# Routing the tokens of a mixture of experts in three units instead of four groups

## The chip, the core and the metric

The kernel is one program on one core of a Trainium2 chip. Its time is the device time of one execution in microseconds (us); 608.5 us is the median of three runs (608.38 to 609.04).

The engines are TensorE (PE, matmuls; its weight loads are listed as PEld), VectorE (DVE), ScalarE (ACT), GpSimd (POOL) and SyncE (SP, which here only issues transfers). Each works through its own list of instructions in order and waits on semaphores for the others.

## The reference: what is computed

Eight sequences of 256 tokens, 128 numbers a token, in fp32, pass four blocks. Each block adds its result to its input and takes a layer norm:

```
x = LN(x + linear_attention(x))      # 16 heads, Taylor features
x = LN(x + two_experts_and_shared(x))# 128 -> 512 -> 128, top 1 of 2
x = LN(x + attention(x))             # 16 heads of 8, rotary, causal softmax
x = LN(x + moe(x))                   # 8 experts, top 2
```

The last block is the one that changes. A gate scores each token for 8 experts; the best two are kept, with a softmax over their two scores. An expert computes `silu(x W1) * (x W2)`, 256 wide, and then `W3` back to 128. The output is the sum of the two experts' answers, weighted.

## The kernel before

**Tiles, groups and slots.** The 2048 tokens are 16 tiles of 128. Four tiles, two sequences, make a group (`NG` = 4 groups of `TG` = 4 tiles). The second half of the program holds the softmax attention, the last three groups of the first experts, and the mixture of experts, whose networks are called the second networks.

**How tokens are routed.** After the attention of a group is normed (`normed1`, L1028), `routed` (L1044) places five pieces: `turn` transposes the group's tokens on PE, `scores` multiplies them with the gate and ranks the 8 scores by comparisons on DVE (`ranks`, L1173), `count` adds up on PE how many tokens each expert has before each token (`counts`, L1227), `places` (L1251) turns this on DVE into a row number for each token and choice and into a list of which expert each tile of rows belongs to, and `chances` (L1201) takes the softmax. `sent` (L1059) then scatters each tile's tokens, once for each of the two choices, with an indirect transfer on POOL (L1062) into a table in DRAM, `slots`. In it the rows of one expert stand together and each expert's part begins at a multiple of 128. n tiles of tokens give 2n tiles of rows, and as many as 7 more are needed for the parts' ends, so the table of a group has `SN = 2*TG + E - 1` = 15 tiles of rows. All 15 are computed whatever the counts are. The tables are filled with zeros at the beginning (`emptied`, L218).

**The second networks.** `networks` (L1322) makes the pieces that compute one table. `rows` (L1340) loads four row tiles from DRAM (256 KB, two such buffers), `turn_in` (L1357) transposes them on PE, `weights` (L1348) loads one expert's first weights, 256 KB, from DRAM for each row tile (five buffers, four ahead; the expert's number is read from the list into a register), `up` (L1372) does the four first matmuls of a row tile and the Silu, and `down` (L1401) the second matmuls for two row tiles (each fp32 matmul is two instructions in the trace). Before step 54 Silu is made from Tanh, and one `up` does one tile; from then on one `up` does two. `down` writes the answers to a table in DRAM. When a group's last `down` is done, `joined` (L1518) places the end: gather each token's two answers with indirect transfers on POOL (L1527), weigh and add them, norm, store. The last group does without answers in DRAM: its rows carry their weight and destination along (`pay`), and one-hot matmuls on PE (`placed_back`, L1458) add them at their tokens.

**The order of the work.** `second_half` (L739) writes the order by hand in steps `s`, six for each sequence's attention, from -14 on. At each step the attention's own matmuls come first (`largest`, `weights`, later `attend1`), then pieces fixed to this step (`at`), then n pieces from a queue, then `at_end` pieces. The queue first holds the first experts' pieces, which are gone at step `FREE` = 24. Networks are put into the queue by `begun` (L1072). Before, group g's are put in at step 12 g + 34, so at 34, 46 and 58, and the last group's at 65:

```
            elif s < LATE:
                n = 2 - s % 2
            elif s < LAST:
                n = -(-left // (LAST - s))
            else:
                n = 3
```

`LATE` is 54 and `LAST` is 65. So from 34 to 53 one and two pieces are taken in turn, from 54 to 64 what is left is spread evenly, and from 65 on three pieces a step of the last group alone. The attention's score matmuls end with step 47. At step 54 the last sequence's attention is turned back, `ended1` (L1006) adds it at 55, and the last group's routing follows at 56 to 64. Up to `LAST` the order of PE, ACT, DVE and SP is this one; POOL's list is made by the framework, which puts a scatter where its row numbers are ready.

Of the kernel before, what the change touches and what calls it, by code (L numbers as in the profile page):

```python
# [21 lines left out]
TG = 4  # L22
# [9 lines left out]
SN = 2 * TG + E - 1  # L32
# [13 lines left out]
C_COS, C_SIN, C_M2, C_M4, C_TRI, C_TWO, C_SEL, C_ONE, C_LOW, C_FULL, C_TILE, C_DEST, C_END = 0, 256, 512, 514, 518, 582, 614, 742, 746, 748, 752, 767, 775  # L46


def shape_constants():
# [22 lines left out]
    c[:, C_FULL : C_FULL + TG] = P * np.arange(TG)  # L72
# [7 lines left out]
def network(  # L80
# [107 lines left out]
    for j in range(4):  # L188
# [19 lines left out]
        dram.tile([SN * P, SW if g == NG - 1 else D], F32, tag=f"slots{g}", name=f"slots{g}")  # L208
        for g in range(NG)
    ]  # L210
    answers = [
        dram.tile([SN * P, D], F32, tag=f"answers{g}", name=f"answers{g}")
        for g in range(NG - 1)
# [4 lines left out]
    def emptied():  # L218
        for t in slots:
            nc.sync.dma_start(  # L220
                t.rearrange("(t p) w -> p t w", p=P),
                empty[:, : t.shape[1]].unsqueeze(1).broadcast_to([P, SN, t.shape[1]]),
            )
# [512 lines left out]
    slot_is, shares = {}, {}  # L736


    def second_half():  # L739
# [266 lines left out]
        def ended1(b):  # L1006
# [18 lines left out]
            if s == 1:  # L1025
                at(slot[0] + 1, normed1, g, spreads(rs[g], f"b{g}"))

        def normed1(g, spread):  # L1028
            pay = None
            if g == NG - 1:  # L1030
                pay = [
                    route.tile([P, TG, SW], F32, tag=f"pay{r}", name=f"pay{g}{r}", bufs=1)
                    for r in range(2)
                ]
                xs[g] = scaled_rows(rs[g], f"b{g}", spread, pay[0][:, :, 0:D])
                nc.scalar.copy(pay[1][:, :, 0:D], xs[g])
            else:
                xs[g] = scaled_rows(rs[g], f"b{g}", spread)
            routed(g, pay, slot[0])
# [4 lines left out]
        def routed(g, pay, s):  # L1044

            turn, scores, chances, count, places = gates(g, xs[g], pay)

            def placed():
                slot_is[g], nets[g] = places()

            late = g == NG - 1
            for i, piece in zip((1, 2, 3, 4, 5) if late else (2, 3, 4, 5, 7), (turn, scores, count, placed, chances)):

                (at if late or piece is not count else at_end)(s + i, piece)
            for t in range(TG):
                at(s + (6 + t // 2 if late else 8 + t), sent, g, pay, t)
            at(s + (9 if late else 12), begun, g)

        def sent(g, pay, t):  # L1059

            for r in range(2):
                i = nc.gpsimd.indirect_dma_start(  # L1062
                    out=slots[g],
                    out_offset=bass.IndirectOffsetOnAxis(
                        ap=slot_is[g][:, t, r : r + 1], axis=0
                    ),
                    in_=pay[r][:, t, :] if pay else xs[g][:, t, :],
                    in_offset=None,
                )
                apart(i, f"slots{g}")  # L1070

        def begun(g):  # L1072
            queue.extend(networks(g, nets[g]))
# [19 lines left out]
        while s < 6 * B or fixed or queue:  # L1093
# [30 lines left out]
            elif s < LATE:  # L1124
                n = 2 - s % 2
# [16 lines left out]
    def gates(g, x3, pay):  # L1142

        got = {}

        def turn():
            dst = route.tile([P, GW], F32, tag="gT", name=f"gT_{g}", bufs=1)
            got["xT"] = transposed(x3, f"g{g}", nc.scalar, dst=dst)

        def scores():  # L1150
            pg = bank(f"pe_{g}")
            for t in range(TG):
# [7 lines left out]
            got["ranks"] = ranks(g, pg)  # L1160

        def count():
            got["counts"] = counts(g, got["ranks"][2])
# [4 lines left out]
            lambda: chances(g, *got["ranks"], pay),  # L1168
            count,
            lambda: places(g, got["counts"], got["ranks"][3]),  # L1170
        )

    def ranks(g, pg):  # L1173
        s = spool.tile([P, TG, E], F32, tag="gs", name=f"gs_{g}")
        nc.vector.tensor_copy(s.rearrange("p t e -> p (t e)"), pg[:, : E * TG])
        shape = [P, TG, E, E]
        other = s.unsqueeze(2).broadcast_to(shape)
        own = s.unsqueeze(3).broadcast_to(shape)
        gt = spool.tile(shape, F32, tag="gt", name=f"gt_{g}", bufs=1)
        nc.vector.tensor_tensor(gt, other, own, ALU.is_gt)  # L1180
        ge = spool.tile(shape, F32, tag="ge", name=f"ge_{g}", bufs=1)
# [5 lines left out]
            cst[:, C_TRI : C_TRI + E * E].unsqueeze(1).broadcast_to([P, TG, E * E]),  # L1187
        )
        nc.vector.tensor_max(gt, gt, ge)
        rank = spool.tile([P, TG, E], F32, tag="rank", name=f"rank_{g}")  # L1190
        nc.vector.tensor_reduce(rank, gt, AX.X, ALU.add)

        chosen = route.tile([P, TG + 1, E], BF16, tag="chosen", name=f"chosen_{g}")
        nc.gpsimd.memset(chosen[:, TG, :], 0.0)
        nc.vector.tensor_single_scalar(chosen[:, 0:TG, :], rank, 2.0, op=ALU.is_lt)
        ranked = route.tile([P, TG, 2, E], F32, tag="ranked", name=f"ranked_{g}")
        for n in range(2):
            nc.vector.tensor_single_scalar(ranked[:, :, n, :], rank, float(n), op=ALU.is_equal)
        return s, rank, chosen, ranked

    def chances(g, s, rank, chosen, ranked, pay):  # L1201
# [509 lines left out]
```

## Time and profile before

| | |
|---|---|
| median of three runs | 608.5 us |
| the profiled execution | 610.6 us |
| its span, first to last instruction | 608.9 us |
| PE busy | 550.6 us, 90% |
| DVE, ACT, POOL busy | 54%, 41%, 25% |
| mean granted clock of PE | 0.954 |
| `up` matmuls, L1384 | 480, 70.1 us busy |
| `down` matmuls, L1408 | 240, 36.8 us busy |
| scatters L1062 and gathers L1527 of the first three groups | 24 and 24, near 1 us each on POOL |
| expert weight loads | 60 of 256 KB |

Times inside the trace count from the first instruction. "Busy" is the union of an engine's instructions in a stretch. Matmuls overlap, so the mean duration of one (300 ns in L1384) is longer than the step from one to the next (146 ns, 70.1 us over 480). The granted clock is the share of full speed that PE's throttle allowed. In a timeline row the bracket holds the idle time before the instruction and what ended it; "issue" is time in which the engine waited for nothing that the profile shows, and "remote" an event whose sender it doesn't know.

### The profile page before, as it was taken

How to read it: one execution, taken by the hardware profiler on the slowest of the kernel's cores; microseconds unless marked ns; L12 is line 12 of the kernel's file. 1: busy time of each engine (PE TensorE's matmuls, PEld its weight loads, DVE VectorE, ACT ScalarE, POOL GpSimd, SP SyncE). 2: the span in 40 equal slices, each digit the busy share in tenths (PEclk: the TensorE clock that was granted, in tenths of full speed). 3: DMA queues.
4: the chain of work that ended last, by engine and by line, in shares of the span. 5: the costliest groups of instructions: out<-in, count | busy, mean ns of one | idle time of the engine just before them, and what ended most of it. 6: DMA issues, size and time to landing. Idle time of an engine off the chain costs nothing.

```text
span 608.9 us, 11095 instructions
## 1 busy us (share of the span) xinstructions
PE 550.6 (90%) x4380; PEld 363.9 (60%) x4380; DVE 329.7 (54%) x773; ACT 251.8 (41%) x370; POOL 152.2 (25%) x185
## 2 busy tenths in 40 slices
PE   8999999999999899999999999789889669667896
PEld 3556666666644544445545554557668559567896
DVE  3364677586662353754655477448636326244464
ACT  4465445545511142344544445254256216034131
POOL 5122211212220210122313113612522540721300
PEclk9899999999998999999899999799889969959999
DMA  9109530232220000000000000402143337547721
GB/s 325 56 2 287 114 71 9 64 72 71 58 82 1 0 2 0 1 1 1 1 1 1 1 1 10 148 23 81 65 135 108 106 124 211 165 138 199 212 58 36
DMA packets 39507, 46.31 MB, mean 76 GB/s; under 512 B 3253, under 2 KB 28488, under 8 KB 38432
## 3 DMA queue, kind: packets, MB, share of 16 engines
q1 hardware_dynamic: 37088, 40.33, 23.6%
q0 software_dynamic: 2080, 4.49, 2.3%
q8 instruction: 35, 0.57, 0.4%
q10 hardware_dynamic: 288, 0.79, 0.4%
q14 instruction: 16, 0.13, 0.1%
HBM read 35.42 MB, written 10.17 MB: 75 GB/s over the span
## 4 chain that ended last, share of the span: by engine, by line
PE 71%; DVE 14%; ACT 5%; issue 5%; another core or an unknown queue 3%; DMA 1%; POOL 0%; DVEq 0%; ACTq 0%
PE pg L1384 8%; PE pf L664 7%; PE ph L646 6%; PE po L516 5%; DVE mx L896 5%; PE py L436 5%; PE sb L933 4%; PE pv L359 4%; PE pd L1408 4%; PE s L397 3%; PE sa L864 3%; PE pa L966 2%; PE pr L793 2%; PE py L444 2%
## 5 line engine op out<-in xcount | busy, mean ns | idle before, releaser
L1384 PE MATMUL pg<-xTs,we 128*128 128x128 f32 x480 | 70.1, 300 | 17.4 <-issue 7.6
L1384 PEld LDWEIGHTS pg<-xTs,we 128*128 128x128 f32 x480 | 64.8, 213 | 21.4 <-issue 8.9
L896 DVE TENSOR_REDUCE mx<-sa 128x4 f32<-128x1024 f32 (+1 forms) x48 | 56.5, 1221 | 30.9 <-PE sa L887 18.7
L945 POOL TENSOR_SCALAR_AFFINE_SELECT pr<-pr 128x512 f32<-128x512 f32 (+1 forms) x48 | 37.7, 794 | 132.1 <-ACT pr L943 132.1
L460 POOL TENSOR_TENSOR y<-y 128x512 f32<-128x512 f32 x32 | 33.3, 1041 | 131.5 <-DVE y L453 103.4
L413 ACT ACTIVATE at<-s,rt_half 128x1536 f32<-128x1536 f32 x32 | 49.1, 1536 | 32.0 <-PE s L405 31.7
L414 DVE SCALAR_TENSOR_TENSOR at<-at,causal 128x1024 f32<-128x1024 f32 x32 | 39.2, 1225 | 40.5 <-ACT at L413 40.3
L943 ACT ACTIVATE pr<-sb 128x1024 f32<-128x1024 f32 x48 | 46.6, 1022 | 27.0 <-PE sb L933 22.4
L933 PE MATMUL sb<-qm,kr 32*128 32x128 f32 (+1 forms) x512 | 36.8, 364 | 11.6 <-DVE mx L896 11.3
L1391 DVE TENSOR_TENSOR hT<-pg,sg 128x512 f32<-128x512 f32 (+1 forms) x24 | 15.4, 645 | 58.0 <-ACT sg L1390 36.1
L1408 PE MATMUL pd<-e,hT 128*128 x240 | 36.8, 292 | 8.4 <-issue 8.0
L436 PE MATMUL py<-at,v 128*64 128x256 f32 x256 | 40.9, 398 | 0.5 <-DVE at L414 0.3
L1390 ACT ACTIVATE sg<-pg 128x512 f32<-128x512 f32 (+1 forms) x24 | 13.4, 561 | 62.4 <-remote 32.9
L933 PEld LDWEIGHTS sb<-qm,kr 32*128 32x128 f32 x512 | 24.3, 197 | 24.6 <-DVE mx L896 22.5
L1408 PEld LDWEIGHTS pd<-e,hT 128*128 128x128 f32 x240 | 32.5, 203 | 9.7 <-issue 8.4
L516 PEld LDWEIGHTS po<-wo_sb,y 128*128 128x128 f32 x256 | 31.8, 191 | 9.7 <-issue 5.7
L664 PE MATMUL pf<-hq,w 128*128 128x512 f32 x72 | 36.5, 597 | 0.0
L516 PE MATMUL po<-wo_sb,y 128*128 128x128 f32 x256 | 33.6, 282 | 1.6 <-DVE y L507 1.6
L359 PE MATMUL pv<-wv,xt 128*128 128x512 f32 x64 | 33.6, 633 | 0.5 <-DVE kT L352 0.5
L1062 POOL DMA_INDIRECT slots<-x_b,slot_i x24 | 23.6, 984 | 30.6 <-DVE nets L1301 24.7
L1527 POOL DMA_INDIRECT yb<-answers,slot_i x24 | 23.1, 963 | 29.8 <-DVE mv_o L289 22.8
L966 PE MATMUL pa<-pr,vaug 128*32 128x128 f32 (+1 forms) x512 | 28.3, 337 | 0.0
(240 smaller groups left out, 962.2 us busy)
## 6 DMA issues: line engine op xcount, KB each, us to landing
we<-in_e SPq DMA_DIRECT2D x60, 256.0 KB
bc<-nr SPq DMA_DIRECT2D x14, 512.0 KB
slots<-empty SPq DMA_DIRECT2D x3, 960.0 KB
answers<-yg SPq DMA_DIRECT2D x21, 128.0 KB
xg<-slots SPq DMA_DIRECT2D x9, 256.0 KB
w<-in_w SPq DMA_DIRECT2D x2, 768.0 KB
xt<-in_xt SPq DMA_DIRECT2D x4, 256.0 KB
x<-in_x SPq DMA_DIRECT2D x4, 256.0 KB
```

The source lines that it names most:

```text
L359: nc.tensor.matmul(pv, xT[:, t * P : (t + 1) * P], wv_sb[:, w], start=True, stop=True)
L413: nc.scalar.activation(at, ps[:, :, 0:SC], AF.Square, bias=rt_half, scale=SQ_SCALE)
L414: nc.vector.scalar_tensor_tensor(at[:, :, 0 : 2 * P], at[:, :, 0 : 2 * P], 0.5, causal.unsqueeze(1).broadcast_to([P, 4, 2 * P]), ALU.add, ...
L436: nc.tensor.matmul(py[o, cc], v[:, 0, w], at[:, i, :].rearrange("p (a q) -> p a q", q=P)[:, 0::2, :], start=True, stop=False,)
L516: nc.tensor.matmul(po, ys[b, c // 2][:, c % 2, q * P : (q + 1) * P], wo_sb[:, c, :], start=(c == 0), stop=(c == 7),)
L664: nc.tensor.matmul(got["o"], w2_sb[:, k * P : (k + 1) * P], hq.pop(n), start=(n == 0), stop=(n == 11),)
L896: nc.vector.tensor_reduce(mx[:, 2 * h : 2 * h + 2, 3 * js.start : 3 * js.stop - 2 : 3], ps[h].rearrange("p i (j k) -> p i j k", j=js.stop ...
L933: nc.tensor.matmul(ps[i // 2][:, i % 2, jj * wd : (jj + 1) * wd], kT[r, j, k], qms[b][r, j // 3, q], start=True, stop=True,)
L943: nc.scalar.activation(w, ps[h], AF.Exp)
L966: nc.tensor.matmul(pa[r, jj, :] if m == 0 else pa[r, jj, P:T], va[:, t + m, 4 * i + j, :], prs[b, jp][:, i, jj * T : (jj + 1) * T] if m == ...
L1384: nc.tensor.matmul(ph[:, b, cw], w[:, cw], x, start=True, stop=True)
L1408: nc.tensor.matmul(po[:, a * P : (a + 1) * P], hT[m][:, a, c * P : (c + 1) * P], e3_sb[:, bass.ds(net_i, 1), c * D : (c + 1) * D].rearrang ...
```

## The change

The mixture is routed in three units of 6, 6 and 4 token tiles: the sequences 0 to 2, 3 to 5, and 6 and 7. Tables have 19, 19 and 15 row tiles. As norms come by group, the work up to the ranks, and the ends, are done in five parts: group 0; the first half of group 1 (both unit 0); the second half of group 1; group 2 (both unit 1); group 3 (unit 2). Each part has its own gate transposes, scores, ranks and chances; counts and places come once a unit, when its last part is ranked; each part has its own gathers, sums, norm and store.

In steps: unit 0's last sequence is normed at step 28, counted at the end of 32, placed at 33 and put into the queue at 40. Unit 1's is normed at 46, counted at the end of 49, placed at 50, and put in at 55. Unit 2 goes as group 3 went. The pacing has a new bound `SECOND` = 55: unit 0's 34 pieces are spread evenly over steps 40 to 54, and from 55 what is left is spread to `LAST` as before.

```diff
+PARTS = [(0, 0, 0, 4, 0), (0, 1, 0, 2, 4), (1, 1, 2, 2, 0), (1, 2, 0, 4, 2), (2, 3, 0, 4, 0)]
+UT = [sum(n for v, _, _, n, _ in PARTS if v == u) for u in range(3)]
+SNS = [2 * n + E - 1 for n in UT]
...
-            if s == 1:
-                at(slot[0] + 1, normed1, g, spreads(rs[g], f"b{g}"))
+            for p, (_, pg, t0, n, _) in enumerate(PARTS):
+                if pg == g and t0 + n == 2 * s + 2:
+                    r = rs[g][:, t0 : t0 + n, :]
+                    at(slot[0] + 1, normed1, p, r, spreads(r, f"b{p}"))
...
-            late = g == NG - 1
-            for i, piece in zip((1, 2, 3, 4, 5) if late else (2, 3, 4, 5, 7), (turn, scores, count, placed, chances)):
-
-                (at if late or piece is not count else at_end)(s + i, piece)
-            for t in range(TG):
-                at(s + (6 + t // 2 if late else 8 + t), sent, g, pay, t)
-            at(s + (9 if late else 12), begun, g)
+            late = u == 2
+            full = off + n == UT[u]
+            when = (1, 2, 5, 3, 4) if late else (1, 2, 6, 3, 4) if u == 1 and full else (2, 3, 7, 4, 5)
+            for i, piece in zip(when, (turn, scores, chances)):
+                at(s + i, piece)
+            if not full:
+                return
+
+            (at if late else at_end)(s + when[3], count)
+            at(s + when[4], placed)
+            tiles = [(q, t) for q, part in enumerate(PARTS) if part[0] == u for t in range(part[3])]
+            for i, (q, t) in enumerate(tiles):
+                at(s + (6 + i // 2 if late else 5 + i // 2 if u == 1 else 6 + i), sent, q, pay, t)
+            at(s + (9 if late or u == 1 else 12), begun, u)
...
-            elif s < LATE:
-                n = 2 - s % 2
+            elif s < SECOND:
+                n = -(-left // (SECOND - s))
...
             if m == n_pairs - 1:
-                joined(g)
+                for p, part in enumerate(PARTS):
+                    if part[0] == unit:
+                        joined(p)
...
         s = slot[0]
-        if s < LATE:
-            s += 3
-            places, sums = (0, 1, 2, 3), (6, 6, 7, 7, 8)
+        if unit == 0:
+            s += 1 + off
+            places, sums, end = (0, 1, 2, 3), (4, 4, 5, 5, 6), 1
         else:
 
-            s = max(s + 1, LATE + 10)
-            places = (0, 0, 0, 0) if g == 1 else (0, 0, 1, 1)
-            sums = (1, 1, 1, 1, 1) if g == 1 else (4, 4, 4, 5, 5)
+            s = max(s + 1, LATE + 10) + off // 2
+            places, sums, end = ((0, 0), (3, 3, 3), 2) if off == 0 else ((0, 0, 1, 1), (4, 4, 5, 5, 5), 2)
         later(s, begin)
         later(s + sums[0], opened)
-        for t in range(TG):
+        for t in range(n):
             later(s + places[t], gathered, t)
             later(s + sums[t], summed, t)
         later(s + sums[-1], spread)
         later(s + sums[-1] + 1, scaled)
-        later(s + sums[-1] + (1 if s < LATE else 3), stored)
+        later(s + sums[-1] + end, stored)
...
+    SECOND = LATE + 1
```

The rest of the diff replaces groups by units or parts in names, shapes and tables: `gates`, `ranks` and `chances` take a part of n tiles, `counts`, `places` and `networks` a unit, and constants grow from 775 to 781 columns.

## Prediction

> **What bounds the kernel now.** I read the table of the engines first: TensorE (PE) is busy 90% of the span, the next engine 54%. Then I cut the second half into stages with the table of stretches, using the order of matmuls to place the program's steps: step 24 starts at 359.5 us, 30 at 391.7, 34 at 405.5, 40 at 433.1, 50 at 469.0, 54 at 479.7, 55 at 489.1, and the last group's own networks (step 65) at 558.3. These are eight of the nine rows of that answer; columns are PE, weight load, DVE, ACT, POOL, then the granted clock, the DMA share and GB/s.
>
> ```profile
> 391.70:405.50 13.80, 12.85 (x131) 7.23 (x129) 6.72 (x11) 5.59 (x8) 3.58 (x5) 0.99 0.13 39
> 405.50:433.10 27.60, 25.86 (x281) 19.45 (x277) 23.10 (x69) 14.61 (x23) 6.15 (x8) 0.94 0.24 70
> 433.10:480.80 47.70, 41.92 (x472) 33.23 (x469) 24.33 (x84) 21.61 (x39) 18.00 (x22) 0.96 0.38 112
> 480.80:499.00 18.20, 9.53 (x58) 8.79 (x57) 1.63 (x4) 3.15 (x6) 11.78 (x12) 0.78 0.31 88
> 499.00:518.20 19.20, 19.20 (x148) 18.93 (x148) 12.83 (x49) 11.95 (x22) 0.03 (x1) 0.85 0.78 225
> 518.20:558.30 40.10, 27.89 (x194) 25.84 (x193) 13.73 (x39) 9.95 (x19) 15.59 (x16) 0.83 0.63 176
> 558.30:576.80 18.50, 13.90 (x103) 13.04 (x102) 8.66 (x29) 5.88 (x10) 7.63 (x8) 0.91 0.59 168
> 576.80:608.90 32.10, 25.51 (x225) 25.00 (x223) 19.16 (x59) 8.13 (x14) 0.00 (x0) 0.97 0.21 60
> ```
>
> Steps 30 to 33 have no network pieces beside the attention and still keep PE busy 12.85 of 13.8 us; where pieces are added, the steps grow by about what these cost. So a piece taken out of any stage is worth its PE time. The exceptions are 480.8 to 499.0 (PE 9.5 of 18.2 us) and 518.2 to 558.3 (27.9 of 40.1). In both, POOL issues 16 indirect transfers back to back at 1.28 us each, and the others stand: the timeline shows PE and ACT resuming as POOL's run ends, and the list of waits has ACT's Silu waiting for something that the profile can't name.
>
> ```profile
> 494.96 0.97 POOL L1527 DMA_INDIRECT yb<-answers,slot_i  x1 [0.30 <-issue]
> ...
> 497.61 0.60 ACT L1390 ACTIVATE sg<-pg 128x512 f32<-128x512 f32 x1 [11.67 <-remote]
> ```
> ```profile
> ACT sg L1390 <- remote: 32.9, 5, 11.7
> ```
>
> I asked for the same columns over each of the five runs of indirect transfers (8, 8, 16, 16 and 8 of them):
>
> ```profile
> 378.30:390.40 12.10, 7.90 (x93) 5.37 (x92) 5.32 (x11) 2.56 (x5) 9.20 (x10) 0.78 0.47 153
> 430.90:443.00 12.10, 9.99 (x121) 7.58 (x119) 5.30 (x13) 1.79 (x5) 9.08 (x10) 0.92 0.20 67
> 475.60:497.00 21.40, 12.79 (x93) 11.37 (x93) 3.16 (x9) 3.01 (x5) 15.74 (x16) 0.86 0.37 108
> 518.20:541.00 22.80, 12.23 (x79) 10.52 (x78) 5.14 (x14) 1.40 (x4) 15.59 (x16) 0.80 0.45 128
> 561.20:574.20 13.00, 10.06 (x69) 9.56 (x70) 3.97 (x12) 3.58 (x7) 7.62 (x8) 0.87 0.58 164
> ```
>
> Span less PE busy gives PE's idle time: 4.2, 2.1, 8.6, 10.6 and 2.9 us. A run of 8 costs 3.1 on average and one of 16 costs 9.6, so each transfer past the eighth costs (9.6 - 3.1) / 8 = 0.81 us. By this line a run of 12 costs 6.3 and one of 24 costs 16.1. I use the line as a rule of this trace without knowing its cause.
>
> The Trainium skill speaks against that reading: "SBUF — State Buffer", section "Who interferes with whom", says that DMA never contends with a compute engine. By it the runs would cost nothing and their rearrangement neither; the measured 8.6 and 10.6 us decide here.
>
> **The change, part by part.** *Fewer tiles.* A unit of n token tiles needs 2n + 7 network tiles: 19 + 19 + 15 = 53 in place of 4 x 15 = 60. Prices at full clock, start to next start in the timeline: one `up` 0.95 us, a tile's `down` 0.47, its transpose 0.14, so 1.56 a tile and 10.9 for seven; by the page's whole groups (70.1/480 x 8 + 36.8/240 x 4 + 0.15) it is 1.93 and 13.5. The stages below spend this saving; it isn't added to them.
>
> *Steps 24 to 39 (359.5 to 433.1).* Before, the first group's networks start at step 34; now they start at 40, since unit 0 waits for the third sequence. Out go 6 `up` and 3 transposes of 4 tiles with a wait of 0.7 and half-clock time: -8.8. The first group's run of 8 goes (-4.2), a run of 12 comes at step 33 (+6.3). Gates: transposes and scores are the same 16 tiles in all, in five parts; the fifth part adds 17 DVE instructions of 0.2 to 0.4 us, two parts being half as wide, against one fewer set of counts and places (13 of 0.2). The attention's matmuls (PE 12.85 of 13.8) hide most; I take +0.2, and +3 if that cover fails. Sum -6.5.
>
> *Steps 40 to 53 (433.1 to 479.7).* Before: 11 `up`, 7.5 pair-`down`, 2 transposes, 18.6 us. Now unit 0's 34 pieces but for the last two go here, three a step in the first four steps: 29.6, so +11.0. The second group's run (2.1) goes. Three pieces a step turn over three PSUM banks behind DVE's 1.2 us reductions; two pieces a step show waits of 0.7 (446.3 us), so I take +1.5 between 0 and +4. Sum +10.4; step 54 starts at 483.6, 3.9 late.
>
> *Step 54 to the first `up` of unit 1.* Here the change adds a wait. The queue is now emptied by step 55, and unit 1's networks are put in it there; their first transposes stand on PE ahead of everything else, the last part's gate transposes of step 57 included. Its counts come at the end of step 49, near 471; the first scatter follows 3.4 us after the counts (472.2 to 475.6 before), near 474; 12 at 1.28 take until 489.5; SP's row fetch starts 1.3 later (441.9 to 443.2 before), 490.8. The trace doesn't show the landing of such a row chunk; the nearest row is a weight tile of the same 256 KB, on which the chain of work waits 4.5 us (548.4 to 552.9). Transposes and copy take 1.3 (407.3 to 408.6): 496.6. That is the low end. But unit 0's gathers (8 and 4) join the scatter to a run of 24, ending near 505, and ACT came back 1.7 after the end of such a run: 506.6 is the high end. I take the middle, 501.6, since PE still moved at 0.7 us an instruction in the old runs. Before, `up` was at speed again at 499.0.
>
> On the clock: the granted clock is 0.78 in 480.8 to 499.0, so such a wait is followed by slow matmuls. The skill's "TensorE: Matmul & The Clock Gate", section "Part 1: The HAM clock gate", says half rate comes after an idle window of about 3.4 us and lasts as long again; an estimate by it is 1.7 us for the new wait. The old wait had the same, so the sum has no term for it.
>
> *Steps 55 to 64.* From 499.0 to 558.3 PE ran 24 `up` tiles and 28 `down` tiles beside a run of 16. Now 19 of each stand beside a run of 8 (the last unit's scatter): 59.3 - 5 x 0.95 - 9 x 0.47 - (10.6 - 3.1) = 42.8. The first weights come with the rows and must land too (PE waited 1.6 for one at 553): +1. So step 65 starts at 501.6 + 43.8 = 545.4, 12.9 earlier. Is the last unit ready by then? Its transposes stand at step 57, after 8 of 34 pieces: +10; scores and counts a step each, +8.6; places 3.4; 8 scatters 10.3; rows and transposes 5.8: 38 us after the restart, below 43.8, and it hides by 6 us.
>
> *After step 65 (50.6 us).* The same 15 tiles and one-hot sums. Unit 1's 12 gathers run here in place of 8: +3.4. The sums and norms of six tiles fall wholly into this stage; those of the old eight began 2 us before it. The chain of work shows them on the path between 581 and 592, so I take +2 between 0 and +5. Sum +5.4.
>
> The total is -12.9 + 5.4 = -7.5 on a span of 608.9: 601.4. The profiled execution took 610.6 us, the span and 1.7 around it; the median of the runs shown is 608.5, 2.1 below. So **601.0 us**.
>
> **Rivals.** *The long run stops everything (slower).* If PE stands for the whole run of 24, and the run ends late because counts stand behind three pieces a step, the restart is not 501.6 but 511 or more. From 509.1 on the gain is gone; at 513 the time is 612.4, and half clock and later gates may bring 618. For it: ACT waited 11.7 us, SP's five weight issues took 14.2. Against: PE did 12.8 of 21.4 us of work in the old run. 0.23.
>
> *The runs cost less.* If unit 0's gathers come after a gap, the run falls into 12 and 12 (12.6, not 16.1), and the restart is at 496.6: -5.0, 596.0; with seven tiles at 1.93 in place of 1.56, another -2.6, 593.4. For it: the gathers need unit 0's last answers, written only after step 54. 0.15.
>
> *The pieces were hidden.* If steps 34 to 39 are held at their length by DVE's maxima (23.1 of 27.6 us busy) the removal gives -2, not -8.8: +6.8, 607.8; for it DVE's share, against it the 3.45 us a step that steps 30 to 33 take. 0.12.
>
> That the tiles aren't saved is no rival: the loops run to 19, 19 and 15.
>
> **How the numbers follow.** The forecast, 597 to 606, has 0.50. Differences of 0.2% (1.2 us) are about what a measurement can tell from none. Faster: 0.50 + 0.15 + 0.05 of the hidden case (607.8, near the bound of 607.3) = 0.70; same, its other 0.07; slower 0.23. The range 592 to 613 takes in the better end, the hidden case and the lower half of the slower case; it leaves out some 0.15.
>
> **What would show it.** Right: 53 network tiles (424 matmuls on the `up` line); step 40's first transposes near 427; a wait of PE at unit 1's first transposes or `up`, ending near 502 beside a run of 24; last-unit networks from 545; last stage near 56 us. Wrong: unit 1 restarting after 509; the last unit's transposes waiting for rows; steps 34 to 39 longer than 4 us each; or the runs of indirect transfers leaving PE at work.

## The result: 614.1 us, slower by 0.8%

The changed kernel took 614.05 us (median of five runs, 612.87 to 615.0) against 608.5 (608.12 to 609.8) for the kernel before: a ratio of 1.0084, 95% interval 1.0066 to 1.0101. The forecast of 601.0 was wrong in sign, and the time lies above the range. The profiled execution took 614.06 us with a span of 612.4 and a mean granted clock of 0.939 (before: 610.6, 608.9, 0.954).

One thing is needed to read all numbers below. The kernels were run in six sessions. The kernel before took 608.5, 609.5 and 609.9 us in three of them and 570.7, 572.5 and 571.1 in the other three, with no overlap. I call the first kind pausing and the second quiet, after what the profiles show; ratios are formed inside one session only.

The work did shrink as the diff says: 424 `up` matmuls for 480, 53 weight loads for 60, PE busy 543.1 us for 550.6. But PE's idle time rose from 58.3 to 69.3 us. First the stages of the changed kernel, from the table of stretches: steps 24 to 39, 40 to 53, 54 to 64, and from 65 on. Columns as in the prediction (PE, weight load, DVE, ACT, POOL, clock, DMA share, GB/s).

```profile
355.60:434.10 78.50, 63.41 (x568) 38.55 (x571) 45.55 (x119) 33.00 (x46) 26.59 (x30) 0.83 0.11 35
434.10:497.90 63.80, 55.27 (x556) 44.18 (x553) 30.85 (x103) 26.62 (x51) 19.11 (x22) 0.89 0.42 121
497.90:552.00 54.10, 36.71 (x285) 33.88 (x283) 24.00 (x88) 21.35 (x37) 19.48 (x20) 0.90 0.55 150
552.00:612.30 60.30, 44.95 (x323) 42.37 (x323) 27.27 (x83) 14.91 (x24) 11.46 (x12) 0.84 0.38 105
```

Before, the same stages took 73.6, 47.1, 78.1 and 50.5 us. So the differences are +4.9, +16.7, -24.0 and +9.8, and -3.9 ahead of step 24, where the two programs do the same work and only the clock differed. They add up to the 3.5 us between the spans. The second and third go together: unit 0's pieces moved out of one stage into the other.

Next, the same table over the five runs of indirect transfers, now 12, 12, 12, 8 and 12 of them:

```profile
401.80:424.00 22.20, 14.54 (x119) 9.53 (x116) 8.94 (x19) 6.41 (x9) 15.20 (x16) 0.65 0.39 120
475.40:496.00 20.60, 13.57 (x80) 8.52 (x81) 4.73 (x18) 2.48 (x6) 11.61 (x12) 0.70 0.35 105
503.70:522.00 18.30, 11.30 (x81) 9.96 (x81) 4.02 (x9) 4.35 (x8) 11.55 (x12) 0.88 0.53 145
537.40:552.00 14.60, 5.49 (x44) 4.82 (x42) 5.70 (x23) 5.87 (x11) 7.93 (x8) 0.87 0.40 110
557.20:577.00 19.80, 11.46 (x77) 9.94 (x76) 4.33 (x11) 4.95 (x7) 11.46 (x12) 0.84 0.63 170
```

Span less PE busy is 7.7, 7.0, 7.0, 9.1 and 8.3 us, 39.1 in sum, against 28.4 over the five runs before. The fourth is not a pause but a wait for the last unit's rows. From the list of PE's waits:

```profile
PE px L1393 <- DMA xg<-slots: 7.9, 1, 7.9
```

A pause looks like this in the timelines of POOL and of ACT: the last scatter of unit 0's run ends at 417.97, and ACT, idle for 6.3 us on an event that the profile can't name, comes back 2 us later.

```profile
417.01 0.96 POOL L1078 DMA_INDIRECT slots<-x_b,slot_i  x1 [0.30 <-issue]
```
```profile
419.97 0.37 ACT L1168 COPY gT<-pt_g 128x256 f32<-128x256 f32 x1 [6.31 <-remote]
```

The section on the kernel before has one thing wrong. Up to `LAST` only PE's order is held by hand (L1613); the lists of ACT, DVE, SP and POOL are placed by the framework there, and it may move a load past others. From `LAST` on all four of PE, ACT, DVE and SP are held. This matters in the experiments on the end.

### The profile page after: what moved, and what is told of

It is laid out like the page before. It is cut to its first block, busy times and chain, and to the rows that moved or that the text cites. A ratio compares the mean times of both kernels' runs of the same rounds, so it can differ in the third digit from the quotient of the medians.

```text
span 612.4 us, 10822 instructions
## 1 busy us (share of the span) xinstructions
PE 543.1 (89%) x4275; PEld 353.6 (58%) x4288; DVE 327.8 (54%) x776; ACT 251.8 (41%) x369; POOL 151.5 (25%) x184
## 4 chain that ended last, share of the span: by engine, by line
PE 69%; DVE 16%; issue 7%; ACT 5%; another core or an unknown queue 1%; DMA 1%; SPq 0%; POOL 0%; DVEq 0%; ACTq 0%
PE pf L668 7%; PE pg L1416 6%; PE ph L650 6%; PE po L520 5%; PE sb L937 5%; DVE mx L900 5%; PE pv L363 4%; PE py L440 4%; PE pa L970 3%; PE s L401 3%; PE sa L868 3%; PE pd L1440 3%; PE pr L797 2%; PE py L448 2%; PE py L1525 2%
## 5 line engine op out<-in xcount | busy, mean ns | idle before, releaser
L1416 PE MATMUL pg<-xTs,we 128*128 128x128 f32 x424 | 59.5, 290 | 11.4 <-issue 7.1
L1416 PEld LDWEIGHTS pg<-xTs,we 128*128 128x128 f32 x424 | 54.4, 204 | 14.4 <-issue 10.4
L418 DVE SCALAR_TENSOR_TENSOR at<-at,causal 128x1024 f32<-128x1024 f32 x32 | 39.1, 1223 | 38.8 <-ACT at L417 38.6
L1440 PE MATMUL pd<-e,hT 128*128 x212 | 32.4, 294 | 5.5 <-issue 2.5
L970 PE MATMUL pa<-pr,vaug 128*32 128x128 f32 (+1 forms) x512 | 32.3, 343 | 5.0 <-issue 4.7
L1440 PEld LDWEIGHTS pd<-e,hT 128*128 128x128 f32 x212 | 28.3, 203 | 8.1 <-issue 4.3
L868 PE MATMUL sa<-kr,rq 32*128 32x384 f32 (+2 forms) x192 | 27.5, 585 | 2.0 <-issue 2.0
L970 PEld LDWEIGHTS pa<-pr,vaug 128*32 128x32 f32 x512 | 14.5, 111 | 24.4 <-issue 14.9
```

The costliest lines, as they stand in the source:

```text
L868: nc.tensor.matmul(o.rearrange("p (j k) -> p j k", j=js.stop - js.start)[:, :n_low, :], qT[r, 0, q], kT[r, js.start : js.start + n_low, k] ...
L970: nc.tensor.matmul(pa[r, jj, :] if m == 0 else pa[r, jj, P:T], va[:, t + m, 4 * i + j, :], prs[b, jp][:, i, jj * T : (jj + 1) * T] if m == ...
L1416: nc.tensor.matmul(ph[:, b, cw], w[:, cw], x, start=True, stop=True)
L1440: nc.tensor.matmul(po[:, a * P : (a + 1) * P], hT[m][:, a, c * P : (c + 1) * P], e3_sb[:, bass.ds(net_i, 1), c * D : (c + 1) * D].rearrang ...
```

## The experiments

**First session (pausing; before 609.49, 605.59 to 613.53).** The first theory was that runs of indirect transfers (the stretches in which POOL issues them back to back) give back what fewer tiles bring. Its rival was that fewer tiles bring little. The first kernel took the tiles alone: the kernel before, which computes only 13, 13 and 12 of the 15 row tiles of its first three groups and writes zeros for the rest's answers.

```diff
...
+        SN = (13, 13, 12, 15)[g]
         n_chunks = -(-SN // TG)
```

> The kernel before, which computes only 13, 13 and 12 row tiles of the first three tables (the 7 last row tiles are left out, their answers are zeros written early) and keeps its four groups and its steps. If a tile's PE time is its price, as the prediction took it, the time falls by 8 to 11 us from 608.5, to 597.5 to 600.5. If the pieces were hidden behind other engines or the pauses, it stays within 2 us of 608.5.

Measured: 607.43 (603.87 to 609.53), ratio 0.9952 (0.9916 to 0.9988). Seven tiles by themselves, with the runs of 16 as they were, bring 0.5% here, far less than the 10.9 us at which I had priced them. Step 65 did come 8 us earlier (550.3 for 558.3), but the last stage then took 55.3 us in place of 50.5.

Two kernels put 24 more scatters, into a table that nobody reads, in the first half of the program. In the first the framework joined what was meant as runs of 4, 8 and 12 to 5 and 19. In the second kernel each transfer's row numbers are first copied on POOL into one of two small tiles, so that a transfer is mostly issued 1.46 us after the last one and not 1.28, and no more than two are on their way at a time.

```diff
+            one = route.tile([P, 1], I32, tag="pone", name=f"pone{k}", bufs=2)
+            nc.gpsimd.tensor_copy(one, col)
+            col = one
+            i = nc.gpsimd.indirect_dma_start(
+                out=spill,
+                out_offset=bass.IndirectOffsetOnAxis(ap=col, axis=0),
...
```

> The kernel before, with three added runs of scatters of constant rows into an unused table, 4, 8 and 12 of them back to back, in steps -13, -9 and -4, where there is no other transfer and POOL has little else. Theory: the run itself stops the others once it is longer than five or so; PE idles under 1 us behind 4, some 3 behind 8, 6 to 8 behind 12, and the whole takes about 10 us longer. Rival: the pauses need the second networks' own loads and waits; then PE idles under 1 us in all three.

> The same three added runs, but each scatter takes its row numbers from one of two small tiles that POOL fills by a copy, so the third can start only when the first is done. Theory of the rate: with gaps between the transfers PE idles under 1 us in all three runs and the time is within 1 us of the kernel before. Rival, a price per transfer: PE idles as behind the back-to-back runs, 0.8 us for each transfer past the fourth or so.

Measured once each: 616.19 and 611.61 us, the second inside the spread of before. With the unspaced run PE waits 1.5 and 3.8 us near its end (the output matmuls after it start at 205.5); with the spaced one no wait beside the run is over 1.2 and the same matmuls start at 198.2. With one execution each the totals are weak; the shift of 7 us inside the traces is larger than the 4.6 us between them, but it too was seen once.

The same spacing went into the changed kernel, for all indirect transfers but the last unit's scatters:

```diff
+    def single(col, name):
+        one = route.tile([P, 1], I32, tag="one", name=f"one_{name}", bufs=2)
+        nc.gpsimd.tensor_copy(one, col)
+        return one
...
+                col = slot_is[u][:, off + t, r : r + 1]
+                if not pay:
+                    col = single(col, f"{p}{t}{r}s")
...
-                    out_offset=bass.IndirectOffsetOnAxis(
-                        ap=slot_is[u][:, off + t, r : r + 1], axis=0
-                    ),
+                    out_offset=bass.IndirectOffsetOnAxis(ap=col, axis=0),
```

> The changed kernel with the same two small tiles of row numbers in all its indirect transfers but the last unit's scatter. Theory of the rate: the idle time of PE behind the four runs of 12 (30 us in the changed kernel's profile) falls below 10, less what later rows and sums cost; 595 to 604 us. Rival, a price per transfer: 612 us or more.

Measured: 595.2 (592.26 to 597.36), ratio 0.9747 (0.9687 to 0.9807), the fastest kernel of any pausing session. The pauses are gone, and the gain lies in steps 40 to 53 (50.8 us for 63.8) and behind step 65 (50.2 for 60.3). Steps 24 to 39 gained nothing (79.7 for 78.5): POOL, busy with the spaced scatters until 425.6, comes late to the attention's masks, and PE stands 7.5 us for one. And a wait stands in the open that the pauses had covered, for unit 1's rows at the first transposes after step 54. From PE's timeline of the paced kernel:

```profile
502.81 1.08 PE L1399 MATMUL px<-ident,xg 128*128 128x128 f32 x4 [12.12 <-DMA xg<-slots]
```

**Second session (quiet; before 570.73, 566.82 to 575.23).** Four kernels were to split that gain: the spacing on the kernel before, the spacing with 38 tiles in three groups (zeros for the rest again), the spacing with six small tiles in place of two, and the spacing with unit 1's networks begun at step 58 in place of 55.

```diff
-    SECOND = LATE + 1
+    SECOND = LATE + 4
-            at(s + (9 if late or u == 1 else 12), begun, u)
+            at(s + (9 if late else 12), begun, u)
```

> The kernel before with the two small tiles of row numbers in all indirect transfers but the last group's scatter. If the pauses come from transfers issued back to back, they are in the kernel before too (28 us of idle PE in five runs, and half clock behind them): 588 to 597 us. If the pacing only repairs what the change broke, 606 to 611 us. Beside after_paced (595) it says what the change is worth without the pauses.

> The paced kernel before, with 13, 13 and 12 row tiles computed in the first three groups (7 tiles left out, zeros in their place). If the seven tiles are worth their PE time and the pauses ate the gain in tiles53, it is 8 to 11 us below before_paced; if the tiles are hidden in any case, within 3 us of it.

> The paced changed kernel with six small tiles of row numbers in place of two: POOL still copies between two transfers, so the step from one to the next stays near 1.46 us, but six may be in flight. Theory of the rate: as after_paced, 592 to 598 us. Rival, the number in flight: the pauses come back, 606 to 614 us.

> The paced changed kernel with unit 0's pieces spread to step 57 in place of 54 and unit 1 put into the queue at 58 in place of 55. If the 12.1 us wait for unit 1's rows and the 7.5 us wait for the last unit's rows in after_paced are real waits for the scatters, both shrink or go and the time is 577 to 589 us. If the later start only moves work to where the last unit's routing then waits, 592 to 600 us.

Measured: 589.07 (ratio 1.0312, 1.0222 to 1.0403), 580.76 (1.0152, 1.0064 to 1.0241), 589.17 (1.0284, 1.0193 to 1.0376) and 599.55 (1.0488, 1.0399 to 1.0577). The expectations were written from the first session, and the kernel before was itself 38 us faster here, so the ratios say little about them: without pauses, spacing only delays the transfers. One comparison inside the session stands: of the two spaced versions of the kernel before, the one with seven tiles fewer is 8.3 us faster (579.43 to 582.03 against 584.21 to 591.07). So in this pair the tiles are worth some 8 us; without the spacing the 53 tiles were not run in a quiet session. Whether it is the spacing or the limit of two on their way that takes the pauses away stays open: the kernel with six small tiles was to tell, but ran only where there are no pauses. Beginning unit 1 later did not help: PE then waited 7.1 us for rows and 12.4 for weights, for a reason that the fourth session shows.

**Third session (quiet; before 572.48, 570.14 to 578.85).** Both kernels again, unchanged, for profiles without pauses, and two more.

> The kernel before, unchanged, for a second profile. The theory (PE stands while POOL works through a run of indirect transfers, and how much of the run it loses differs from chip to chip): the idle time of PE over its five runs goes with its time; at about 609 us it is again near 28 us, at about 571 us it is below 10. The rival (the 38 us between the two chips are the granted clock alone): the idle time is near 28 us in either case and PE's busy time differs by the whole of it.

> The changed kernel, unchanged. Both theories where the kernel before takes about 609 us: 0.5 to 1.2% slower again. Where it takes about 571 us they part. The theory (the runs of twelve transfers give back what the eleven us of tiles bring): no pauses there, so it is 1 to 2% faster than before. The rival (routing six tiles at once makes PE wait for unit 1's and the last unit's rows, 8 to 12 us each, whatever the transfers do to PE): it is 1 to 3% slower.

> The changed kernel with unit 1's networks begun three steps later (58 instead of 55) and unit 0's spread to 58. The theory: a wait for unit 1's rows goes where there was one, the runs of transfers stay, and more pieces are left for the last stage; within 0.5% of the changed kernel where there are pauses. The rival (the wait for unit 1's rows is what costs): 1 to 2% below the changed kernel where PE does not pause in the runs, since the wait of 12 us is then open.

> The changed kernel with the row numbers of each indirect transfer (but for the last unit's scatter) copied first into one of two small tiles, so that POOL issues a transfer only when the second last one has read its numbers. Where the kernel before takes about 609 us: 2 to 3.2% faster than it again, with no pause over 4 us in the runs (both theories). Where it takes about 571 us: the theory has 1 to 3% slower than the unpaced changed kernel (the pacing only lengthens the runs and so the waits for rows); the rival, that pacing does something other than take pauses away, has it faster there as well.

Measured: 574.75 (one run), 587.14 (584.33 to 588.58; ratio 1.0253, 1.0212 to 1.0294), 591.05 (1.0341, 1.0291 to 1.0391) and 595.77 (1.0416, 1.0367 to 1.0465). The expectation for `after_later` fell: the wait for unit 1's rows went to 1.0 us, and one of 14.2 us for weights took its place. The paced kernel takes the same time in both kinds of session, 595.2 and 595.8, where the unpaced ones move by 27 to 38 us. That fits two kinds that differ only in what the unspaced runs do to the engines; one kernel in one session of each kind doesn't prove it. Over the kernel before's five runs, in the quiet session:

```profile
377.90:390.10 12.20, 11.24 (x132) 7.47 (x130) 8.72 (x19) 4.61 (x7) 10.27 (x12) 1.00 0.49 152
425.50:437.60 12.10, 11.72 (x152) 9.48 (x145) 8.46 (x22) 4.67 (x10) 10.17 (x12) 1.00 0.18 67
463.40:484.80 21.40, 19.02 (x165) 17.23 (x165) 12.22 (x40) 11.79 (x19) 15.75 (x16) 1.00 0.48 146
499.90:522.00 22.10, 19.72 (x171) 19.09 (x170) 11.72 (x34) 8.80 (x15) 15.45 (x16) 1.00 0.91 271
528.70:540.00 11.30, 9.62 (x82) 9.11 (x81) 5.60 (x14) 2.84 (x6) 7.61 (x8) 1.00 0.72 218
```

The idle time is 1.0, 0.4, 2.4, 2.4 and 1.7 us, 7.9 in sum for 28.4, beside the same transfers on POOL at the same 1.28 us. The clock is full. Both halves of what was expected hold in part: of the 35.8 us between the two spans of before, 20.4 are idle time and 15.4 are PE's busy time at a lower clock (550.6 to 535.2).

But the changed kernel is slower there too, by 2.5%. My theory had expected 1 to 2% faster without pauses, and fell; the rival's 1 to 3% slower was met. The four stages again, the kernel before in the quiet session and then the changed kernel:

```profile
359.20:426.10 66.90, 61.37 (x636) 39.56 (x636) 47.37 (x123) 33.58 (x49) 22.81 (x27) 1.00 0.20 63
426.10:467.20 41.10, 39.45 (x471) 31.64 (x467) 25.20 (x87) 21.83 (x39) 18.23 (x21) 1.00 0.44 131
467.20:525.10 57.90, 49.08 (x398) 46.87 (x398) 28.78 (x93) 25.26 (x44) 28.28 (x29) 0.94 0.74 222
525.10:573.00 47.90, 37.89 (x325) 36.52 (x324) 27.77 (x86) 14.22 (x24) 7.61 (x8) 0.99 0.36 109
```
```profile
358.40:431.70 73.30, 61.91 (x569) 37.24 (x569) 47.03 (x118) 32.94 (x46) 26.42 (x30) 0.88 0.12 37
431.70:482.40 50.70, 48.85 (x556) 41.47 (x553) 30.81 (x103) 26.90 (x51) 14.71 (x18) 1.00 0.46 136
482.40:536.00 53.60, 36.72 (x285) 34.70 (x283) 24.18 (x88) 21.23 (x37) 23.74 (x25) 0.86 0.56 168
536.00:586.00 50.00, 40.16 (x323) 38.44 (x323) 27.39 (x83) 15.00 (x24) 11.49 (x12) 0.94 0.41 127
```

The differences are +6.4, +9.6, -4.3 and +2.1. The first stage has 67 matmul records fewer and is longer: PE's idle time doubles (5.5 to 11.4 us) and the clock falls to 0.88. Cut into steps 24 to 29, 30 to 33 and 34 to 39, the kernel before and then the changed one:

```profile
359.20:385.70 26.50, 23.65 (x231) 13.75 (x232) 18.91 (x50) 12.86 (x20) 11.28 (x14) 1.00 0.21 63
385.70:400.10 14.40, 13.45 (x132) 7.49 (x130) 6.88 (x13) 6.19 (x9) 6.69 (x8) 1.00 0.17 52
400.10:426.10 26.00, 24.27 (x281) 18.33 (x277) 21.58 (x63) 14.53 (x23) 4.84 (x7) 1.00 0.22 70
```
```profile
358.40:388.70 30.30, 25.23 (x226) 15.24 (x227) 18.30 (x41) 16.54 (x23) 6.78 (x8) 0.92 0.00 1
388.70:404.80 16.10, 14.21 (x145) 8.71 (x143) 12.04 (x39) 5.72 (x9) 2.74 (x5) 0.93 0.00 1
404.80:431.70 26.90, 22.47 (x206) 13.29 (x202) 16.69 (x40) 10.68 (x15) 16.90 (x19) 0.81 0.31 99
```

So steps 34 to 39, out of which the pieces went, are no shorter (+0.9), and 5.5 of the 6.4 us lie ahead of them, where no piece went out and the extra part came in. In the third stage PE works 36.7 of 53.6 us: two waits for rows, 14.4 us in sum (6.7 at unit 1's first transposes, 7.7 at the last unit's), stand where the kernel before had 7.8 for weights. Over the whole program PE's busy time hardly falls, 535.2 to 534.8 us, though it has 92 matmul records fewer; the granted clock is 0.959 for 0.984.

One of the new waits in the first stage has a cause that I had not priced, in the timeline of all engines. The extra part's norm (part 1, normed at step 28) needs a square root amid the attention's exponentials:

```profile
380.23 1.28 ACT L295 ACT_TABLE_LOAD   x1
...
381.52 0.29 ACT L295 ACTIVATE sd_b<-mv_b,eps_ln 128x2 f32<-128x2 f32 x1
...
381.85 0.17 DVE L284 RECIPROCAL rs_b<-sd_b 128x2 f32<-128x2 f32 x1 [1.78 <-ACT sd_b L295]
...
382.57 2.35 DVE L900 TENSOR_REDUCE mx<-sa 128x4 f32<-128x1024 f32 x2
382.91 1.28 ACT L947 ACT_TABLE_LOAD   x1
383.84 0.54 PE L937 MATMUL sb<-qm,kr 32*128 32x128 f32 x4 [2.41 <-DVE mx L900]
```

ACT loads its table twice. DVE waits 1.8 us for the square root's result with the attention's maxima (`mx`) queued behind it, and PE waits 2.4 us for these; the clock goes to half at 384.2. The kernel before has no table load in that place. On the cost, the Trainium skill, "ScalarE: Activation LUTs", section "What ACT_TABLE_LOAD costs", gives 1.283 us and another 1.38 to drain for each switch; the 1.28 agree, but no drain shows here, since the square root starts 1.29 us after the start of the load.

**Fourth session (quiet; before 571.05, 567.18 to 576.54).** Theory A put the loss on the two waits for rows, theory B on steps 24 to 54. Two kernels pace the end so that the last unit's routing has fewer pieces ahead of it (`after_last`; `after_later_last` begins unit 1 at step 58 too), one is the control on the kernel before, and one fills the odd steps 29 to 39 with dummy matmuls.

```diff
-    FREE, LATE, LAST = 24, 6 * (B + 1), 6 * (B + 1) + 11
+    FREE, LATE, LAST = 24, 6 * (B + 1), 6 * (B + 1) + 16
-            at(s + (9 if late or u == 1 else 12), begun, u)
+            at(s + (14 if late else 9 if u == 1 else 12), begun, u)
```
```diff
-    STEADY = {23: 6, 24: 8, 27: 6}
+    STEADY = {23: 6, 24: 8, 27: 6, 29: 6, 31: 6, 33: 6, 35: 6, 37: 6, 39: 6}
```

> The changed kernel with the last unit's networks begun five steps later (70 instead of 65), and unit 1's pieces spread to there, so that fewer of them stand ahead of the last unit's routing (steps 56 to 64) and more behind it. Theory A (what the change loses where PE does not pause is its two waits for rows, 7.7 and 6.7 us at steps 55 and 65): the second wait goes, 1 to 1.5% below the changed kernel on the same sort of chip, so some 1.2% slower than before where before takes about 571 us, and about as fast as before where it takes 609. Theory B (the loss is in steps 24 to 54, where the attention sets the pace and nothing fills PE): the wait goes but the time stays within 0.5% of the changed kernel's.

> As after_last, and unit 1's networks begun at step 58 too, with unit 0's spread to 58. Theory A: both waits for rows go, and with them the wait of 14 us for weights that stood behind the last unit's rows in SP's queue; 2 to 3% below the changed kernel, so as fast as before or up to 1% faster than it where before takes about 571 us. Theory B: at best 1% below the changed kernel, still 1 to 2% slower than before.

> The control: the kernel before with the same edit as after_last (last group begun at step 70, pieces spread to there). It had no wait for rows, only 8.2 us for weights in steps 54 to 64, so both theories expect it within 0.5% of before. If it gains 1% or more, the gain of the two runs above is not the price of the change's waits but a better pacing of the end that the kernel before could have as well.

> The changed kernel with six dummy matmuls (1.46 us of PE by the rows of those that both kernels have at steps 23, 24 and 27) at the odd steps 29 to 39, where no networks are left to fill PE. Theory A: no gain; 0 to 1% slower than the changed kernel. Theory B in the form that PE's idle stretches there cost granted clock (half speed for 17 us between 384 and 425 us, none before): no half speed between 375 and 430 us, the stage from step 24 to 40 shorter by 3 to 6 us, 0.5 to 1% below the changed kernel.

Measured: 590.09 (ratio 1.0313, 1.0247 to 1.0379), 588.22 (1.0257, 1.0187 to 1.0327), 571.07 (0.9975, 0.9941 to 1.001) and 585.45 (1.0242, 1.0179 to 1.0306). Theory A fell: the first two kernels gained nothing on the changed kernel's 1.0253. The control stayed at the kernel before, as expected. In `after_last` the last wait shrank to 2.4 us and the last stage grew from 50.0 to 55.5. In `after_later_last` the waits for rows went to 1.2 us and another of the same size took their place, as the timeline of all engines shows:

```profile
514.54 1.00 POOL L1078 DMA_INDIRECT slots<-pay,slot_i  x1 [0.30 <-DVE rs_o L284]
...
525.85 0.38 SPq L1375 DMA_DIRECT2D xg<-slots  x1
...
531.03 1.22 PE L1416 MATMUL pg<-xTs,we 128*128 128x128 f32 x4 [16.29 <-DMA we<-in_e]
```

Unit 0's twelve gathers filled POOL from 499.3 to 514.2, and the last unit's scatters began right behind them. SP, which takes its list in order, stood from 507.7 to 525.9 at the fetch of these rows, which the framework had placed ahead of unit 1's weight loads. PE had unit 1's rows and no weights.

`after_steady` kept the clock at full speed through the first stage, which took 71.8 us with the dummy matmuls in it, 1.5 below the changed kernel of the third session (theory B had 3 to 6) and 4.9 above before:

```profile
355.10:426.90 71.80, 62.32 (x600) 35.55 (x607) 45.58 (x120) 33.08 (x46) 26.60 (x30) 1.00 0.12 38
```

The 1.5 us are rather a lower bound for what half speed costs, as the dummy matmuls add time of their own: steps 30 to 33 took 17.9 us for 16.1, with PE waiting 1.6 and 0.7 ahead of them, while steps 24 to 29 and 34 to 39 took 28.7 for 30.3 and 25.2 for 26.9. So at full clock, too, steps 34 to 39 are only 0.8 us shorter than with the pieces in them (with three of the six sets of dummy matmuls, some 4.4 us of PE, in their place), and the chain of work back through them in the changed kernel runs over the attention's maxima (25% of it), its scores and exponentials, the norm and the gate's ranks. The whole kernel's ratio can't be told from the changed kernel's 1.0253.

**Fifth session (pausing; before 609.88, 604.38 to 613.22).** Theory A2 was that the end loses to two queues in order, SP's and POOL's. Both kernels have `SECOND` 58, `LAST` 68 and the dummy matmuls, and load the last unit's rows through POOL's queue; the second also moves unit 0's gathers behind the last unit's scatters.

```diff
-            nc.sync.dma_start(
+            (nc.gpsimd if last else nc.sync).dma_start(
                 xg[c][:, :k, :],
...
-            s += 1 + off
+            s = max(s + 1, LATE + 15) + off // 2
```

> The changed kernel with unit 1's networks begun at step 58, the last unit's at 68, dummy matmuls at the odd steps 29 to 39, and the last unit's rows loaded through POOL's queue instead of SP's, so that no weight load stands behind them. Where before takes about 571 us, theory A2 (the end loses to two queues in order: weights behind the last unit's rows on SP, 16.3 us in after_later_last, and the last unit's scatters behind unit 0's twelve gathers on POOL): the wait for weights goes, a wait for the last unit's rows of up to 8 us comes in its place; 577 to 583 us, 1 to 2% slower than before. Theory B2 (the order of the queues only moves the wait about, PE lacks work there whatever comes first): within 0.5% of the changed kernel, so 2 to 3% slower than before.

> As after_rows_pool, and unit 0's gathers and sums moved to step 69, behind the last unit's scatters on POOL. Theory A2: the last unit's rows land some 12 us earlier, no wait over 3 us is left in steps 54 to 68; 568 to 575 us where before takes about 571, within 1% of it on either side. Theory B2: within 0.5% of after_rows_pool.

Measured: 621.92 (618.39 to 624.95; ratio 1.0215, 1.0153 to 1.0277) and 617.44 (615.54 to 618.13; 1.0136, 1.008 to 1.0192). The expectations were for a quiet session. What carries over is the step from the first to the second: step 68 begins at 548.5 for 562.6, with no wait for rows or weights among the larger ones in either kernel. But only 4.5 us of the 14 reach the end, since the 24 gathers now run in the last stage (65.3 us for 54.5). The largest wait of both is a pause behind unit 1's twelve scatters; in PE's timeline of the second:

```profile
496.24 1.54 PE L988 MATMUL pyt<-ident,ya 128*128 128x128 f32 x6 [11.40 <-ACT ya L982]
```

No version beat both kernels in both kinds of session: in a pausing one the spaced kernel is the fastest, in a quiet one the kernel before. The spaced 53-tile version of the kernel before (580.8 us in a quiet session) was not run in a pausing one and doesn't compute the reference.

## Why the prediction was wrong, step by step

Up to the first `up` of unit 1 the sum came out, and by luck: 502.5 us against 501.6. Step 54 began some 14 us late (497.9 for 483.6), and the 18 us forecast from there to the restart shrank to 4.6. From there, step 65 came at 552.0 against 545.4, and the last stage took 60.3 against 56.0 (50.6 and 5.4). So of the 11.0 us by which the span missed 601.4, 0.9 lie before that `up`, 5.7 between it and step 65, and 4.4 after.

- **"So a piece taken out of any stage is worth its PE time."** This reading failed, and with it **"Steps 24 to 39 ... Sum -6.5"**: the stage grew by 4.9 us, and by 6.4 in the quiet session. Taking out the pieces of steps 34 to 39, priced at -8.8, brought +0.9 there. Before, the pieces of steps 34 to 39 stood in the gaps of the attention's chain from scores to maxima to weights; in the third session that stretch took 26.0 us with them and 26.9 without. I had this as the third rival, at 0.12, and dismissed it because steps 30 to 33 have few gaps at PE busy 12.85 of 13.8 us. A dense PE in one stretch did not show that the next is bound by PE. The fifth part was taken at +0.2; its norm brings two table loads and a wait of 2.4 us with it, and steps 24 to 33, where it stands, grew by 5.5 us in the quiet session. How much of this is the part itself and how much the lower clock is not shown.
- **"Steps 40 to 53 ... Sum +10.4."** The work was priced rightly: +9.6 where nothing pauses. In the predicted session it was +16.7, as unit 1's scatters (idle 7.0 us) fell into this stage instead of the next.
- **"A run of 24", ending near 505.** There was none: unit 0's gathers waited for its last answers, so the run fell into 12 and 12, as the second rival had it. Unit 1's transposes found their rows landed, since PE came to them late; its rows were not what set 501.6. In the sessions without pauses, and with spacing, PE is early and the wait stands in the open (6.7 and 12.1 us).
- **"It hides by 6 us."** Wrong, and the main miss behind the restart: the last unit's rows came 7.9 us late. The fill was near its 43.8 us (its last `down` ended at 544.1, 42.5 after the forecast restart), but the routing, summed to 38 us, took over 50. Beside unit 0's twelve gathers PE all but stood from 512 to 521, ahead of and amid the last unit's gate transposes, so these ended near 521.3, 20 us after the restart and not 10; and places took 6.9 us, not 3.4, as DVE had unit 0's sums and norms between them. Scores and counts (9.3 us), scatters (10.1) and rows (6.3) came about as forecast. The last transpose behind the pause, in PE's timeline:

```profile
520.92 0.37 PE L1166 MATMUL pt_g<-ident,pay 128*128 128x128 f32 x1 [1.73 <-issue]
```

Without pauses the wait was as long (7.7 us in the quiet session), with places at 6.9 us there too.

- **"+5.4" after step 65.** The mechanism was right and the size not: +9.8, for the run of twelve gathers leaves PE idle for 8.3 us, not 6.3, and the stage's clock is 0.84 where before it was 0.95. Without pauses the stage grew by 2.1.
- **The line for runs.** Twelve transfers cost 7.0 to 8.3 us where the line gave 6.3. As a rule of that trace it was near; as a rule of the chip it does not hold, since in the profile of a quiet session the same runs cost 0.4 to 2.4.
- **Seven tiles at 10.9 us.** 8.3 where they were taken out with spacing, 2.1 (0.5%) without it in a pausing session. The tiles' price was not the main miss: the change moves the remaining work to where PE is full (steps 40 to 53) and away from where it has gaps (24 to 39, 54 to 64).

The rival on the slower side ("the long run stops everything") had the right sign by a mechanism that did not occur. What the runs show in its place is a schedule with fewer, larger units: each waits longer for its last member, its transfers come in longer blocks, and PE has nothing else to do meanwhile. That this is the cause of the whole quiet loss of 14.7 us is supported by the stages, not shown by one kernel that undoes it: each attempt moved the wait to the next queue. Open too is why unspaced runs stop PE, ACT and DVE in some sessions and not in others; the packets of the indirect transfers took about the same time in both (105 and 102 ns on average). It does not go by the chip's number alone: the record gives chip 5 for the first session and for the fourth, one of each kind. And the profiles differ in another way: none of the eight pausing ones gives a time to landing for any transfer, all twelve quiet ones do, also for the paced kernel, whose time is the same in both. So an event "that the profile can't name" may be a gap in its records, and whether these have to do with the pauses was not tested.

## What to carry to other kernels

Work taken out of a stretch is worth its engine time only if that engine sets the stretch's length; test this with the chain of waits of that very stretch, not with its neighbour's busy share. Joining small units to larger ones saves padding, but each larger unit starts later and comes in longer blocks, so look for what fills the engine until then, and for what is queued behind the block on each queue that works in order. A time read from one session can hold a disturbance of the session: run both versions side by side in more than one before trusting a per-event price.

## What the runs showed of the hardware that I had not expected

- Beside runs of 8 to 16 indirect transfers on POOL, 1.28 us apart, PE idled for 2.1 to 10.6 us each in the kernel before's profile of a pausing session (ACT for up to 11.7), and for under 2.5 in that of a quiet one. In the changed kernel with the transfers 1.46 us apart and at most two on their way the pauses were gone, and its time was the same in both kinds (595.2 and 595.8 us). The Trainium skill, "SBUF — State Buffer", section "Who interferes with whom", has it that transfers never contend with compute engines and that PE and ACT wait on nobody. The quiet profile, with 0.4 to 2.4 us a run, is near that; the idle time in the pausing one is not explained by it, and as no run here names the cause, contention is not shown either.
- Idle time is not the whole price of pauses: the same kernel's PE busy time was 550.6 us at a granted clock of 0.954 and 535.2 at 0.984, so 15.4 us of PE time came on top of 20.4 us of idle time.
- A row fetch that waits at the head of SP's list held back weight loads for other work by 18 us.
